# A decoder layer: the third part of the attention weights kept in memory, and the first batch's weight work moved to other engines

## The chip, the cores and the metric

The kernel runs on one core of a Trainium2 chip. The metric is device time in microseconds (us), as a median of three runs. A profile comes from one further execution and has its own time. The engines are named as in the profile: PE is TensorE, which multiplies matrices (PEld its weight loads, which overlap with it); DVE is VectorE; ACT is ScalarE; POOL is GpSimd; SP is SyncE, which here only issues transfers (DMAs). DMAs are carried by 16 DMA engines, whichever engine issued them: SP's are in queue q1 of the profile, ACT's in q10, POOL's in q0. When a line says L209, it is line 209 of the kernel before.

## The reference

The layer is computed for 4 batches of 512 rows with 512 columns, in float32. Cut to what matters:

```python
x = x + attention(layernorm(x))          # 16 heads of 128; Wq, Wk, Wv: [512, 2048], Wo: [2048, 512]
x = x + gamma * cross(layernorm(x), ctx) # 8 heads of 64 with softmax over 512 columns, no weights
x = x + ffn(layernorm(x))                # hidden size 1365; w1, w3, w2 made ternary with a mean-|w| scale
```

Inside the attention each head's score matrix is 128 x 128 (the sequence is contracted away), softmax runs over its last axis, and `att @ v` is turned back and multiplied with `Wo`. The change concerns the attention's weights alone.

## The kernel before

**Attention, by batch and by head group.** Batches run one after the other. Within a batch there are four head groups j, of four heads each. A group does four products in this order: `pu` (the rows of x against Wo), `py` (the Gram matrix G of x against Wk), `pm` (Wv against the result u of `pu`) and the scores `sc` (Wq against the result y of `py`). Softmax (`e`), its transpose (`pe`, evicted as `eT`) and the output product `po` of group j run inside group j+1: `pe` in the middle of `py`, `po` after it (`midway` and `output` in the loop at L637).

**The first batch is different from the others.** Batch 0 multiplies plain float32 weights (`products_f32`, L275). `first_weights` (L197) loads them in four chunks of 128 rows, as 512-byte pieces for q, k and v and as 2 KB rows for o. From each chunk of q, k and v it subtracts the last row of the weight matrix, which it has loaded as a broadcast tile `last`; this is a POOL operation, L209. The last row of the last chunk is then overwritten with the bias by a 2 KB load, L212, which waits for L209.

`keep_weights` (L216) cuts each chunk t of k, v and o into a high part h = t x constant (ACT, L223) and a low part l = t - S x h (DVE, L225) and stores both: h from ACT's queue (L224), l from POOL's queue (L226). A chunk of q is stored as it is, from ACT's queue (L219). That makes 24 + 4 stores of 256 KB a head group.

Batches 1 to 3 use the parts in three faster products (`products`, L242): h with h, l with l, and a difference part d with d. `weights` (L228) loads h and l on SP's queue and remakes d = l - h on POOL (L236). Products of h and l come first and that of d after them, for two row blocks at a time.

**Buffers.** Chunks and parts share a ring of 18 tiles of 256 KB (`a_w`, L134), so a load waits until the tile that lies 18 back is no longer used. In the first batch the parts h and l lie in a pool of six buffers each (`first`, L622). Its memory is given to the cross attention's input pool afterwards: the first loads of that pool (`keys`, L528) wait for all of the first pool's stores, and the loads of batch 1's x follow them on SP's queue.

**Evictions.** `evict` (L310) copies a PSUM bank to SBUF, in turn on ACT (L313) and DVE (L315). It is used by the products of batch 0 and by the Gram matrix of every batch.

**Order of the work.** The framework lays out each engine's instructions when the kernel is built, and an engine runs its own list strictly in order: an instruction that waits holds up everything behind it on that engine, transfers in its queue too. In the built list ACT has the copies of G and u behind the h of the next group's o chunk, which waits for that chunk's load. Within the attention of batches 1 to 3, steps of the preceding batch's cross attention and of the ternary quantization (`abs_w`, `tern_w`) are put in between by ticks; the first loads of the quantization are listed within batch 0. The FFN comes last and is not touched.

Of the kernel before, what the change touches and what calls it, by code (L numbers as in the profile page):

```python
# [10 lines left out]
F32 = mybir.dt.float32  # L11

F32R = mybir.dt.float32r
BF16 = mybir.dt.bfloat16
AF = mybir.ActivationFunctionType
ALU = mybir.AluOpType
AX = mybir.AxisListType

P = 128
B, T, D = 4, 512, 512  # L20
NC = T // P
KC = D // P
DH = 128
NG, HG = 4, 4
GW = HG * DH
# [7 lines left out]
S = 4096.0  # L33
H_OF = 1.0 - 0.5**13
# [3 lines left out]
def decoder_layer_kernel(  # L38
# [16 lines left out]
    nc = tc.nc  # L55
# [74 lines left out]
    def apool(name, bufs):  # L130
        return apools.enter_context(tc.tile_pool(name=name, bufs=bufs))
# [4 lines left out]
    yp, stp, tp = apool("a_y", 5), apool("a_stage", 2), apool("a_t", 3)  # L136
# [3 lines left out]
    kept_q = [dram.tile([D, GW], F32, name=f"kept_q_{j}") for j in range(HG)]  # L140
    kept = {
        (n, j, part): dram.tile([D, GW], F32, name=f"kept_{n}{part}_{j}")
        for n in "kvo"
        for j in range(HG)
        for part in "hl"
    }

    class Side:
# [29 lines left out]
    def load(dst, src):  # L178
        nc.sync.dma_start(dst, src)
        return dst  # L180

    def wtile(name, dt=F32R):
        return wp.tile([P, GW], dt, tag="w", name=name)

    w_of = {"q": wq, "k": wk, "v": wv}

    def heads(t):
        return t.rearrange("p (g c) -> p g c", g=NG)

    def of_heads(w, j):  # L190

        return w[:, :, ts(j, DH)].rearrange("g p c -> p g c")

    def by_group(rows, g):
        return rows.rearrange("(p g) d -> g p d", g=NG)[g]

    def first_weights(n, j, first):  # L197

        if n != "o":
            last = first.tile([P, GW], F32, tag="last", bufs=2, name=f"{n}_last_{j}")  # L200
            load(heads(last), of_heads(w_of[n][:, D - 1 : D, :], j).to_broadcast([P, NG, DH]))
        chunks = []
        for k in range(KC):
            t = wtile(f"{n}_raw_{j}_{k}", F32)
            if n == "o":
                load(t, by_group(wo[j * T : (j + 1) * T, :], k))
            else:
                load(heads(t), of_heads(w_of[n][:, ts(k, P), :], j))
                nc.gpsimd.tensor_tensor(t, t, last, ALU.subtract)  # L209
                if k == KC - 1:  # L210
                    bias = bqkv[:, ts(KINDS.index(n), GW)].rearrange("(o g) c -> g o c", o=1)
                    load(heads(t[P - 1 : P, :]), of_heads(bias, j))  # L212
            chunks.append(t)
        return chunks

    def keep_weights(n, j, chunks, first):  # L216
        for k, t in enumerate(chunks):
            if n == "q":
                nc.scalar.dma_start(kept_q[j][ts(k, P), :], t)  # L219
                continue  # L220
            h = first.tile([P, GW], F32R, tag="h", name=f"{n}_h_{j}_{k}")
            l = first.tile([P, GW], F32R, tag="l", name=f"{n}_l_{j}_{k}")
            nc.scalar.mul(h, t, H_OF / S)  # L223
            nc.scalar.dma_start(kept[n, j, "h"][ts(k, P), :], h.bitcast(F32))  # L224
            nc.vector.scalar_tensor_tensor(l, h.bitcast(F32), -S, t, ALU.mult, ALU.add)  # L225
            nc.gpsimd.dma_start(kept[n, j, "l"][ts(k, P), :], l.bitcast(F32))  # L226

    def weights(n, b, j):  # L228
        if n == "q":
            return [load(wtile(f"q_{b}_{j}_{k}", F32), kept_q[j][ts(k, P), :]) for k in range(KC)]  # L230
        tris = []
        for k in range(KC):
            tri = Tri(*(wtile(f"{n}{p}_{b}_{j}_{k}") for p in "hld"))
            load(tri.h.bitcast(F32), kept[n, j, "h"][ts(k, P), :])
            load(tri.l.bitcast(F32), kept[n, j, "l"][ts(k, P), :])
            nc.gpsimd.tensor_tensor(  # L236
                tri.d, tri.l.bitcast(F32), tri.h.bitcast(F32), ALU.subtract
            )
            tris.append(tri)
        return tris  # L240

# [33 lines left out]
    def products_f32(name, lhs, rhs, done, midway=None):  # L275

        for i in range(4):
            if i == 2 and midway:
                midway()
            p = bank(f"{name}_{i}")  # L280
            for k in range(4):
                nc.tensor.matmul(  # L282
                    p, lhsT=lhs(k)[:, ts(i, P)], rhs=rhs(k), start=(k == 0), stop=(k == 3)
                )
            done(i, p)
# [19 lines left out]
            tris.append(tri)  # L305
        return xs, tris

    turn = [0]

    def evict(dst, src):  # L310
        turn[0] += 1
        if turn[0] % 2:
            nc.scalar.copy(dst, src)  # L313
        else:
            nc.vector.tensor_copy(dst, src)  # L315

    def gram_upper(b, xs):
        if b == 0:
# [17 lines left out]
    def gram_rest(b, G):  # L336

        for rows in ((1, 2), (3,)):
            pt = bank(f"gt_{b}_{rows[0]}")
            n = 0  # L340
            for j in rows:
                for i in range(j):
                    nc.tensor.transpose(pt[:, ts(n + i, P)], G[i][:, ts(j, P)], ident)
                evict(G[j][:, : j * P], pt[:, n * P : (n + j) * P])
                n += j
        tris = []
        for m in range(KC if b > 0 else 0):
            tri = Tri(*(g3p.tile([P, D], F32R, name=f"g{p}_{m}") for p in "hld"))
            tri_of(tri, G[m])
            tris.append(tri)  # L350
        return tris
# [71 lines left out]
    def turned(b, j, e):  # L423
        eT = ep.tile([P, NG, DH], F32, tag="eT", bufs=2, name=f"eT_{b}_{j}")
        transpose_blocks(eT, e, f"pe_{b}_{j}", True)
        return eT

    def output(b, j, eT, ms, accs):
        for g in range(NG):
            po = bank(f"po_{b}_{j}_{g}")  # L430
            nc.tensor.matmul(po, lhsT=eT[:, g, :], rhs=ms[g], start=True, stop=True)  # L431
            if b == 0:
                nc.vector.tensor_tensor(accs[g], po, accs[g], ALU.add)
            else:
                nc.vector.scalar_tensor_tensor(accs[g], po, S * S, accs[g], ALU.mult, ALU.add)
            if j == HG - 1:
                (nc.gpsimd if b == B - 1 else nc.sync).dma_start(by_group(x_a[b], g), accs[g])
# [184 lines left out]
    first = first_pools.enter_context(tc.tile_pool(name="first", bufs=6, side="right"))  # L622
    cpools = ctx.enter_context(ExitStack())

    def accumulators(b):
        accs = []
        for g in range(NG):
            acc = accp.tile([P, D], F32, tag="acc", name=f"acc_{b}_{g}")
            load(acc, by_group(x[b], g))
            nc.gpsimd.tensor_tensor(acc, acc, bo_bc, ALU.add)  # L630
            accs.append(acc)
        return accs
# [4 lines left out]
    for j in range(HG):  # L637
        us, ys, ms = {}, {}, {}

        def to(tiles, pool, tag, name):  # L640
            def done(i, p):
                tiles[i] = pool.tile([P, 512], F32, tag=tag, name=f"{name}_{i}")
                evict(tiles[i], p)

            return done

        def midway():
            if waiting:
                waiting[2] = turned(*waiting[:3])

        w = first_weights("o", j, first)
        products_f32(
            f"pu_0_{j}", lambda c: xs[c], lambda c: w[c], to(us, u3p, "u3", f"u_0_{j}")
        )
        if j == 0:
            gram_rest(0, G)
        keep_weights("o", j, w, first)
        w = first_weights("k", j, first)
        products_f32(
            f"py_0_{j}", lambda e: G[e], lambda e: w[e], to(ys, yp, "y", f"y_0_{j}"), midway  # L660
        )
        keep_weights("k", j, w, first)
        if waiting:
            output(*waiting)
        w = first_weights("v", j, first)
        products_f32(f"pm_0_{j}", lambda k: w[k], lambda k: us[k], to(ms, mp, "m", f"m_0_{j}"))
        keep_weights("v", j, w, first)
        w = first_weights("q", j, first)
        e = scores(0, j, w, ys)
        keep_weights("q", j, w, first)  # L670
        if j == 0:
            load(bo_bc, bo.to_broadcast([P, D]))
            load(gam, gamma.to_broadcast([P, 1]))
            accs = accumulators(0)
        if j == HG - 1:
            xs, x3 = normed(1, False)
        waiting = [0, j, e, ms, accs]
# [8 lines left out]
    for b in range(1, B):  # L686
# [10 lines left out]
        for j in range(HG):  # L697
# [3 lines left out]
            ys = keys_of(b, j, g3, weights("k", b, j), tick)  # L701
# [62 lines left out]
    for i in range(NHC):  # L764
        r = min(P, HID - i * P)
# [3 lines left out]
    for b in range(B):  # L769
# [3 lines left out]
        for i in range(NHC):  # L773
# [4 lines left out]
            r = min(P, HID - i * P)  # L778
# [25 lines left out]
        for c in range(NC):  # L804
# [3 lines left out]
            for i in range(NHC):  # L808
                r = min(P, HID - i * P)
# [59 lines left out]
```

## Time and profile before

| | us |
|---|---|
| median of 3 runs (lowest to highest) | 1261.23 (1254.18 to 1262.58) |
| the profiled execution: its time / its span | 1263.35 / 1261.6 |
| batch 0 of the attention, to the end of its last `po` | 0 to 253 |
| batches 1 to 3 with cross attention and quantization | 253 to 950 |
| FFN | 950 to 1262 |

| stretch | PE busy | DVE | ACT | POOL | granted PE clock | DMA share | GB/s |
|---|---|---|---|---|---|---|---|
| 0 to 64 us | 37.4 | 31.4 | 15.7 | 33.6 | 0.81 | 0.96 | 324 |
| 64 to 119 us | 52.4 | 20.3 | 14.3 | 21.9 | 1.00 | 0.79 | 257 |
| 119 to 253 us | 133.0 | 57.3 | 32.2 | 47.5 | 0.99 | 0.60 | 197 |
| 253 to 950 us | 674.1 | 502.2 | 259.6 | 204.2 | 0.99 | 0.60 | 196 |
| 950 to 1262 us | 305.3 | 151.5 | 132.7 | 24.5 | 1.00 | 0.16 | 53 |

Busy times are in us. "DMA share" is the mean over the 16 DMA engines: one engine busy alone gives 1/16. A DMA shows in the profile as packets, one for each contiguous piece, with small ones for its end markers; packets are counted by size. "Busy" for PE says that a matmul was in the pipe, not that PE was at its peak. Lines of waits read: who waited <- for whom: us in total, times, the longest.

### The profile page before, as it was taken

To read this page: it belongs to the slowest core of one execution; us is meant where nothing else is said; L and a number is where in the kernel's file an instruction comes from. 1 tells how busy PE (TensorE), PEld (TensorE's weight loads), DVE (VectorE), ACT (ScalarE), POOL (GpSimd) and SP (SyncE) were. 2 spreads that over 40 slices of the span, in tenths; PEclk is the share of its full clock that TensorE was granted. 3 is DMA by queue.
4 is the path that set the end of the run, shared out by engine and by line. 5 is a ranking of instruction groups with operands and counts; after the bars stand their busy time and mean duration, and the time that the engine had idled before them with its cause. 6 is when DMAs were issued, how large, how long until landed. Compare 5 with 4: busy or idle time off the path is not lost.

```text
span 1261.6 us, 15663 instructions
## 1 busy us (share of the span) xinstructions
PE 1202.1 (95%) x5182; PEld 812.9 (64%) x5182; DVE 762.6 (60%) x1411; ACT 454.5 (36%) x948; POOL 331.6 (26%) x306
## 2 busy tenths in 40 slices
PE   7499999999999999999999999999999999999998
PEld 3153544577675666777675677776766666678786
DVE  6334336387786864975969475686856845635232
ACT  3113222134332432352334334332534836724020
POOL 5535343143321322432222243222302000000000
PEclk9699999999999999999999999999999999999999
DMA  9978675284476654743775374557765120020101
GB/s 311 334 243 292 234 242 198 81 269 150 147 230 214 196 167 147 255 151 131 230 244 178 128 243 150 168 199 241 238 212 188 42 75 26 9 92 17 53 15 51
DMA packets 137401, 214.19 MB, mean 170 GB/s; under 512 B 13156, under 2 KB 56212, under 8 KB 137320
## 3 DMA queue, kind: packets, MB, share of 16 engines
q1 hardware_dynamic: 122664, 178.58, 44.2%
q0 software_dynamic: 5440, 17.83, 3.9%
q10 hardware_dynamic: 9216, 16.78, 3.5%
q8 instruction: 41, 0.67, 0.2%
q14 instruction: 40, 0.33, 0.1%
HBM read 162.81 MB, written 50.33 MB: 169 GB/s over the span
## 4 chain that ended last, share of the span: by engine, by line
PE 79%; DMA 10%; DVE 6%; issue 2%; ACT 1%; POOL 1%; SPq 1%; ACTq 0%; DVEq 0%; POOLq 0%
PE h L784 13%; PE y L811 6%; PE xo L586 5%; PE xs L542 5%; PE sc L394 4%; PE xp L106 4%; PE py L282 4%; PE pm L282 3%; PE po L431 3%; PE pu L282 2%; PE pg L326 2%; DMA o_raw<-in_wo_dram 1%; DMA v_raw<-in_wv_dram 1%; PE pm_2h L249 1%; DMA kl<-kept_kl 1%
## 5 line engine op out<-in xcount | busy, mean ns | idle before, releaser
L784 PE MATMUL h<-fxh,t 128*128 128x512 f32 (+1 forms) x352 | 140.4, 401 | 0.8 <-ACT fxh L116 0.8
L784 PE MATMUL h<-fxl,t 128*128 128x512 f32 (+1 forms) x352 | 138.3, 395 | 0.0
L554 ACT ACTIVATE p<-xs,xnmax 128x512 f32<-128x512 f32 x128 | 87.0, 687 | 88.5 <-DVE xnmax L549 43.6
L236 POOL TENSOR_TENSOR od<-ol,oh 128x512 fp32r<-128x512 f32 x48 | 62.9, 1310 | 203.7 <-DMA ol<-kept_ol 56.1
L548 DVE TENSOR_REDUCE xnmax<-xs 128x1 f32<-128x512 f32 x128 | 83.9, 682 | 29.9 <-PE xs L542 29.7
L236 POOL TENSOR_TENSOR vd<-vl,vh 128x512 fp32r<-128x512 f32 x48 | 67.5, 1412 | 114.5 <-DMA vl<-kept_vl 66.2
L236 POOL TENSOR_TENSOR kd<-kl,kh 128x512 fp32r<-128x512 f32 x48 | 63.9, 1332 | 121.3 <-DMA kl<-kept_kl 67.3
L784 PEld LDWEIGHTS h<-fxh,t 128*128 128x128 f32 (+1 forms) x352 | 65.1, 185 | 20.0 <-issue 1.5
L542 PE MATMUL xs<-keys,qs 64*128 64x512 f32 x256 | 75.9, 641 | 0.8 <-DVE u L270 0.8
L784 PEld LDWEIGHTS h<-fxl,t 128*128 128x128 f32 (+1 forms) x352 | 65.0, 185 | 15.7
L106 PE MATMUL xp<-ident,p 128*128 128x128 f32 x512 | 66.9, 275 | 4.2 <-DVE u L270 4.2
L566 DVE TENSOR_SCALAR p<-p,xrden 128x512 f32<-128x512 f32 x128 | 68.3, 575 | 3.0
L106 PEld LDWEIGHTS xp<-ident,p 128*128 128x128 f32 x512 | 59.1, 141 | 16.5 <-DVE u L270 4.7
L811 PE MATMUL y<-t,gh 128*128 128x512 f32 (+1 forms) x176 | 69.5, 395 | 0.0
L811 PE MATMUL y<-t,gl 128*128 128x512 f32 (+1 forms) x176 | 68.8, 391 | 0.0
L118 POOL CAST gh<-gf 128x512 fp32r<-128x512 f32 (+1 forms) x24 | 14.8, 616 | 197.1 <-DVE gf L795 174.1
L431 PE MATMUL po<-m,eT 128*128 128x512 f32 x128 | 60.3, 614 | 6.3 <-ACT eT L109 5.7
L586 PE MATMUL xo<-pt,vals 128*64 128x512 f32 x256 | 63.7, 599 | 2.5 <-ACT pt L109 2.4
L282 PE MATMUL py<-k_raw,G 128*128 128x512 f32 x128 | 60.4, 626 | 4.3 <-issue 4.3
L109 ACT COPY pt<-xp 128x512 f32<-128x512 f32 x96 | 53.4, 593 | 27.1 <-PE xp L106 27.1
L795 DVE SCALAR_TENSOR_TENSOR gf<-h,scales_w,sl 128x512 f32<-128x512 f32 (+1 forms) x44 | 32.9, 747 | 47.2 <-PE h L784 39.3
L282 PE MATMUL pu<-o_raw,xn 128*128 128x512 f32 x128 | 55.6, 592 | 0.0
(215 smaller groups left out, 2559.2 us busy)
## 6 DMA issues: line engine op xcount, KB each, us to landing
oh<-kept_oh SPq DMA_DIRECT2D x48, 256.0 KB
ol<-kept_ol SPq DMA_DIRECT2D x48, 256.0 KB
kh<-kept_kh SPq DMA_DIRECT2D x48, 256.0 KB
kl<-kept_kl SPq DMA_DIRECT2D x48, 256.0 KB
vh<-kept_vh SPq DMA_DIRECT2D x48, 256.0 KB
vl<-kept_vl SPq DMA_DIRECT2D x48, 256.0 KB
q<-kept_q SPq DMA_DIRECT2D x48, 256.0 KB
t_w<-tern_w SPq DMA_DIRECT2D x24, 227.5 KB
```

The costliest lines, as they stand in the source:

```text
L106: nc.tensor.transpose(pt[:, ts(k, P)], src[:, ts(k, P)], ident)
L109: nc.scalar.copy(dst, pv)
L236: nc.gpsimd.tensor_tensor(tri.d, tri.l.bitcast(F32), tri.h.bitcast(F32), ALU.subtract)
L282: nc.tensor.matmul(p, lhsT=lhs(k)[:, ts(i, P)], rhs=rhs(k), start=(k == 0), stop=(k == 3))
L431: nc.tensor.matmul(po, lhsT=eT[:, g, :], rhs=ms[g], start=True, stop=True)
L542: nc.tensor.matmul(sc, lhsT=qs[rows, ts(m, P)], rhs=keys[rows, :], start=True, stop=True)
L548: nc.vector.reduce_max(nmax[:, j : j + 1], scs[j], axis=AX.X)
L554: nc.scalar.activation(p, scs[j], AF.Exp, bias=nmax[:, j : j + 1], scale=xscale, accum_out=den[:, j : j + 1],)
L566: nc.vector.tensor_scalar(ps[j], ps[j], rden[:, j : j + 1], None, ALU.mult)
L586: nc.tensor.matmul(po[rows, :], lhsT=vals[:, l, rows], rhs=pt[j][:, l, :], start=(l == 0), stop=(l == NC - 1),)
L784: nc.tensor.matmul(ph[:r, :], lhsT=t[:, k, i * P : i * P + r], rhs=fxT[j][:, k, :], start=(k == 0 and j == 0), stop=(k == KC - 1 and j == 1),)
L811: nc.tensor.matmul(py, lhsT=g[i][j][:r, ts(c, P)], rhs=t2[:r, i, :], start=(i == 0 and j == 0), stop=(i == NHC - 1 and j == 1),)
```

## The change

Four things are done at once.

- `keep_weights` also makes d = l - h and stores it, and `weights` loads d as it loads h and l. POOL no longer remakes it.
- In batch 0, the subtraction of the last row, h, l and d are all DVE operations. The h and l operations of `keep_weights` are followed by stores that all go out from POOL's queue, q's too.
- `evict` always uses ACT.
- In head group 1 two one-column DVE copies take both buffers of the quantization's staging pool, after y is there. Its loads (`abs_w`) wait for them.

One thing more follows from the order of the bias: the last chunk of q, k and v is loaded as 127 rows and one row, and the subtraction runs on 127 rows. The bias load no longer waits for a subtraction.

In the built lists, a head group of batch 0 now has 40 stores on POOL's queue (12 h, 12 l, 12 d, 4 q) and none on ACT's; a head group of batches 1 to 3 has 40 loads on SP's queue, where it had 28, each d behind its h and l.

```diff
@@ -142,7 +142,7 @@
         (n, j, part): dram.tile([D, GW], F32, name=f"kept_{n}{part}_{j}")
         for n in "kvo"
         for j in range(HG)
-        for part in "hl"
+        for part in "hld"
     }
 
     class Side:
@@ -205,25 +205,33 @@
             if n == "o":
                 load(t, by_group(wo[j * T : (j + 1) * T, :], k))
             else:
-                load(heads(t), of_heads(w_of[n][:, ts(k, P), :], j))
-                nc.gpsimd.tensor_tensor(t, t, last, ALU.subtract)
-                if k == KC - 1:
+                r = P if k < KC - 1 else P - 1
+                load(heads(t[:r, :]), of_heads(w_of[n][:, k * P : k * P + r, :], j))
+                if r < P:
                     bias = bqkv[:, ts(KINDS.index(n), GW)].rearrange("(o g) c -> g o c", o=1)
-                    load(heads(t[P - 1 : P, :]), of_heads(bias, j))
+                    load(heads(t[r:, :]), of_heads(bias, j))
+                nc.vector.tensor_tensor(t[:r, :], t[:r, :], last[:r, :], ALU.subtract)
             chunks.append(t)
         return chunks
 
     def keep_weights(n, j, chunks, first):
+        def keep(name, part):
+            nc.gpsimd.dma_start(name[ts(k, P), :], part)
+
         for k, t in enumerate(chunks):
             if n == "q":
-                nc.scalar.dma_start(kept_q[j][ts(k, P), :], t)
+                keep(kept_q[j], t)
                 continue
-            h = first.tile([P, GW], F32R, tag="h", name=f"{n}_h_{j}_{k}")
-            l = first.tile([P, GW], F32R, tag="l", name=f"{n}_l_{j}_{k}")
-            nc.scalar.mul(h, t, H_OF / S)
-            nc.scalar.dma_start(kept[n, j, "h"][ts(k, P), :], h.bitcast(F32))
-            nc.vector.scalar_tensor_tensor(l, h.bitcast(F32), -S, t, ALU.mult, ALU.add)
-            nc.gpsimd.dma_start(kept[n, j, "l"][ts(k, P), :], l.bitcast(F32))
+            h, l, d = (
+                first.tile([P, GW], F32R, tag=p, name=f"{n}_{p}_{j}_{k}").bitcast(F32)
+                for p in "hld"
+            )
+            nc.vector.tensor_scalar(h.bitcast(F32R), t, H_OF / S, None, ALU.mult)
+            keep(kept[n, j, "h"], h)
+            nc.vector.scalar_tensor_tensor(l.bitcast(F32R), h, -S, t, ALU.mult, ALU.add)
+            keep(kept[n, j, "l"], l)
+            nc.vector.tensor_tensor(d.bitcast(F32R), l, h, ALU.subtract)
+            keep(kept[n, j, "d"], d)
 
     def weights(n, b, j):
         if n == "q":
@@ -231,11 +239,8 @@
         tris = []
         for k in range(KC):
             tri = Tri(*(wtile(f"{n}{p}_{b}_{j}_{k}") for p in "hld"))
-            load(tri.h.bitcast(F32), kept[n, j, "h"][ts(k, P), :])
-            load(tri.l.bitcast(F32), kept[n, j, "l"][ts(k, P), :])
-            nc.gpsimd.tensor_tensor(
-                tri.d, tri.l.bitcast(F32), tri.h.bitcast(F32), ALU.subtract
-            )
+            for p in "hld":
+                load(getattr(tri, p).bitcast(F32), kept[n, j, p][ts(k, P), :])
             tris.append(tri)
         return tris
 
@@ -305,14 +310,8 @@
             tris.append(tri)
         return xs, tris
 
-    turn = [0]
-
     def evict(dst, src):
-        turn[0] += 1
-        if turn[0] % 2:
-            nc.scalar.copy(dst, src)
-        else:
-            nc.vector.tensor_copy(dst, src)
+        nc.scalar.copy(dst, src)
 
     def gram_upper(b, xs):
         if b == 0:
@@ -672,6 +671,11 @@
             load(bo_bc, bo.to_broadcast([P, D]))
             load(gam, gamma.to_broadcast([P, 1]))
             accs = accumulators(0)
+        if j == 1:
+
+            for i in range(2):
+                held = stp.tile([P, 512], F32, tag="stage", name=f"held_{i}")
+                nc.vector.tensor_copy(held[:, 0:1], ys[i][:, 0:1])
         if j == HG - 1:
             xs, x3 = normed(1, False)
         waiting = [0, j, e, ms, accs]
```

## The prediction

> **What bounds the kernel now.** First the page: span, slices and DMA packets.
>
> ```profile
> span 1261.6 us, 15663 instructions
> ...
> PE   7499999999999999999999999999999999999998
> ...
> PEclk9699999999999999999999999999999999999999
> DMA  9978675284476654743775374557765120020101
> ...
> DMA packets 137401, 214.19 MB, mean 170 GB/s; under 512 B 13156, under 2 KB 56212, under 8 KB 137320
> ```
>
> PE is busy in nearly every slice; only the first two are thin, and there the DMA engines are full. So what can be won lies in batch 0. The waits of 0 to 64 us say what PE lacks there:
>
> ```profile
> ACT o_h L223 <- DMA o_raw<-in_wo_dram: 18.1, 4, 11.3
> ...
> PE gt L343 <- ACT G L313: 13.9, 1, 13.9
> ```
>
> ACT stands before the h of the next group's o chunk until that chunk lands, and the copies of G stand behind it; PE waits 13.9 us, and 4.3 more for the next copy. The stretches by engine confirm it (us, then busy us of PE, PEld, DVE, ACT, POOL, then clock, DMA share, GB/s):
>
> ```profile
> 35.00:49.00 14.00, 0.18 (x1) 0.00 (x0) 2.05 (x4) 1.95 (x4) 8.54 (x8) 0.61 0.97 343
> ...
> 140.00:190.00 50.00, 50.00 (x155) 25.08 (x154) 19.97 (x30) 13.37 (x28) 23.92 (x26) 1.00 0.78 255
> ```
>
> From 119 us on PE has no gap. A head group then takes 48.6 us (the chain has `pu` at 142.05 and again at 190.69). In batches 1 to 3 PE idles 23 of 697 us, shared among many small waits:
>
> ```profile
> PE pm_2h L249 <- DVE acc L435: 4.4, 3, 2.9
> ...
> PE py_0h L249 <- DMA kh<-kept_kh: 4.1, 3, 1.8
> ```
>
> **The change part by part.** The working is against the profiled execution: 1263.35 us, 1.75 over its span and 2.1 over the median.
>
> *ACT is freed.* The h operations (48 x 0.63 = 30 us) and 64 DMA issues leave ACT; the copies of G then follow PE directly. The 13.9 and 4.3 us go: -18 at most.
>
> *POOL and DVE.* POOL loses 48 subtractions (64.1 us, L209) and 144 remakes (194.3 us, L236). It gains 48 stores, and 64 come from ACT: 40 a head group at 0.56 us (L226) = 22 us. DVE gets, by head group, 12 x (0.69 for l by L225 + 0.54 for h by L100 + 2 x 0.69 for subtraction and d by L172) = 31 us, and keeps some 7 for `po` and softmax, against PE's 48.6. This is hidden under PE as long as its inputs arrive. DVE executes in order: an h that waits for a store of six chunks ago holds up the next chunk's subtraction, and then PE.
>
> *Batches 1 to 3.* 144 more loads of 256 KB on SP, 37.7 MB in 697 us: 196 GB/s becomes 250, below the 324 to 343 seen. Each d load waits in SP's queue until PE leaves the old d tile, and the next chunk's h and l are behind it. In group 1 of batch 1 the load of the fourth kh would issue near 309, not at 305.68, and is needed at 314.4; `kl` took 3.7 to 4.2 us to land where PE waited for it, so a margin of 1 to 2 us is left. If that cover fails, 36 products lose up to 0.5 us each: +18. Against it, DVE is rid of POOL's operations beside it (L172 takes 0.78 us here, 0.68 where POOL is quiet). PE's waits for DVE are some 15 us in all; I take back a third. The gram's evictions, now all on ACT, follow PE at 0.6 us. Sum -3, between -15 and +18.
>
> *The 127-row loads.* The largest term, and the diff's smallest line. How many DMA engines carry a load? Two rows of the list of DMAs are of odd shape:
>
> ```profile
> abs_w<-in_w2t_dram SPq DMA_DIRECT2D x1, 170.0 KB
> ...
> k_raw<-in_bqkv_dram SPq DMA_DIRECT2D x4, 2.0 KB
> ```
>
> The first is one of four 85-row DMAs, the second the bias: one row, four pieces. If each engine that took part leaves one small packet at the end, the 809 other 128-row DMAs on the three queues leave 16 x 809 = 12944, and `gam` 128 four-byte pieces and 16. Of the page's 13156 under 512 B, 68 remain for 12 bias loads and four of 85 rows. From 200.7 to 201.4 us one bias load is alone in q1:
>
> ```profile
> DMA packets 34, 0.06 MB, mean 82 GB/s; under 512 B 15, under 2 KB 19, under 8 KB 34
> ...
> q1 hardware_dynamic: 8, 0.00, 1.3%
> ```
>
> Eight packets: its 19 - 15 = 4 pieces and 4 markers. So 12 x 4 = 48, and 20 remain: 5 for each 85-row DMA. The number of engines is then 16 for 128 rows, 4 for 4, 5 for 85, each time the largest divisor up to 16. 127 is prime: one engine. The trace has no such load, so the ends are sixteen engines (0.8 us) and one.
>
> [...]
>
> What one engine moves in such pieces shows from 171.6 to 173.2 us, where only 512-byte pieces are moving:
>
> ```profile
> DMA packets 1060, 0.53 MB, mean 330 GB/s; under 512 B 29, under 2 KB 1060, under 8 KB 1060
> ```
>
> 330 / 16 = 20.6 GB/s an engine; 127 x 2 KB = 260 KB take 12.6 us. The other end is the mean of 0 to 250 us:
>
> ```profile
> q1 hardware_dynamic: 40336, 30.69, 41.6%
> q10 hardware_dynamic: 9216, 16.78, 17.8%
> ```
>
> q10's 64 stores took 17.8% of 16 x 250 us, 11.1 engine-us each, 0.69 on each engine. q1's 1664 engine-us, less 44.5 loads at 11.1 and 14 quantization loads at 9.9, leave 1030 for 60 of these: 17.2 each, with contention. I take 12.6, the row of pure traffic.
>
> Bill of the loaded engine by head group: three 127-row loads 37.8; nine other chunks and three broadcasts, 12 x 0.8 = 9.6; four o loads and 40 stores, 44 x 0.69 = 30.4. Sum 77.8 us, against 40 if spread and PE's 48.6. Four groups 311; x, `acc`, `bo` and batch 1's x, 13 x 0.69 = 9; 14 quantization loads 9; start 3: 332. Less 10 for the last stores, behind which no product waits; with the first slices' share of 0.96 the last q chunk lands at 322 / 0.95 = 339. Then subtraction and `sc` (4 us), the wait of batch 1's x behind the stores with its normalization (7 more), gram, `pe` and `po` (13.5): the last `po` of batch 0 ends at 364, not 253. **+111**, from +94 (no slack) to +162 (17.2 a load). The 18 us from ACT are within: PE waits for loads anyhow. Its clock falls in gaps (0.61 above), but even at half clock a product of 13.7 us fits in the 26 us between two chunk sets.
>
> Sum: 1263.35 + 111 - 3 = 1371; I say 1370.
>
> **The rivals.**
>
> *The short load spreads out* (faster, the other side). For it: nothing here shows 127 rows. Against: 85 rows went to 5 engines; a split by remainder would use 16. Then a group moves 59 x 256 KB = 15.5 MB, 47 us at 330 GB/s, below PE's 48.6; the G stall goes (-18), stores that gate DVE return 3: 1263 - 15 - 3 = 1245. By the bill above, 40 + 37.8/k on k engines, it decides from k = 5 on.
>
> *The stores' queue is the limit.* POOL issues 40 stores in order, each waiting for parts from DVE. At 0.56 us they take 22 us a group; were each delayed by one DVE operation of 0.69, 50 us, just over PE's 48.6. That eats the gain: 1260, about as before. For it: all stores in one queue. Against: issues lasted 0.54 to 0.69 us while DVE was running.
>
> [...]
>
> *The one engine is slower still*: 17.2 us a load and every d load late: 1263 + 162 + 15 = 1440.
>
> **How the numbers follow.** One engine, in the bill's range: 0.88, of which 0.06 for the last rival. Spread out: 0.08. Store queue: 0.04. The time is the bill's, 1370. Low end: 1263 + 94 - 15 = 1342, less 32 because loads may overlap better with stores than one bill allows; high end 1440. 1310 to 1440 leaves out both small rivals and some tail. Faster by over 1% (what a measurement of this kernel can just tell): 0.08; within 1%: 0.04; slower: 0.88.
>
> **What the profile after would show.** Under 512 B: 13156 + 16 x 192 new DMAs - 12 x 15 = 16048 if 127 rows take one engine, 16228 if sixteen. Batch 0 with a DMA share well below 0.96 while PE idles, its gaps ended by the fourth chunk of k, v and q, three times a group; `po` of the groups 75 to 90 us apart. No wait for G behind o_h. No L236; loads of d beside h and l, and PE's waits for them under 10 us. I am wrong if the gaps end with DVE behind stores, or if batch 0 ends before 253.

## The result, and the profile after

The changed kernel takes 1380.51 us (median of 4 runs, 1379.01 to 1384.17); the kernel before took 1261.90 beside it (1254.18 to 1263.97). The ratio is 1.0949, with a 95% interval of 1.0901 to 1.0997: it is **slower by 9.5%**, 119 us. The forecast was 1370, from 1310 to 1440.

The page of the changed kernel, with the rows that answer to those shown of before: span, then the 40 slices of TensorE, of its granted clock and of the DMA engines, then the packets.

```profile
span 1380.1 us, 15677 instructions
...
PE   7862185383999999999999999999999999999998
...
PEclk9986597697899999999999999999999999999999
DMA  6674455664477677769667776957796412002101
...
DMA packets 157652, 264.50 MB, mean 192 GB/s; under 512 B 16048, under 2 KB 59056, under 8 KB 157572
```

Three things are to be seen. The gaps of TensorE lie in the first ten slices (34.5 us each), all within batch 0; behind them the row is nines. In these same slices the DMA engines are only four to seven tenths busy, where they were seven to nine tenths busy in the first four before: TensorE lacks data while the DMA engines, taken together, have time. And the packets under 512 bytes are exactly the 16048 that the prediction had worked out for a 127-row load on one engine (sixteen engines would have left 16228).

Stretches by engine tell it in time (from:to, us, then busy us of PE, PEld, DVE, ACT, POOL, then clock, DMA share, GB/s). Two lie in batch 0, the third covers batches 1 to 3:

```profile
0.00:64.00 64.00, 48.68 (x120) 23.07 (x121) 29.81 (x71) 10.95 (x22) 19.69 (x39) 0.95 0.63 211
...
119.00:200.00 81.00, 35.52 (x95) 16.94 (x94) 30.83 (x61) 9.80 (x22) 22.11 (x40) 0.71 0.56 194
...
395.00:1071.00 676.00, 667.90 (x3154) 472.84 (x3153) 451.07 (x932) 261.98 (x618) 18.46 (x16) 1.00 0.75 255
```

Of the 81 us from 119 to 200, which TensorE filled before (80.65), it now works 35.5, at a clock of 0.71. The DMA share there is 0.56.

Where batch 0 ends can be read from the last addition of a head group's output (`acc<-po`). It starts at 252.8 us before and at 393.8 after: +141. From there to the last such addition of batch 3 it is 699.7 us before (to 952.5) and 677.2 after (to 1071.0): -22.5. The rest, 309 us, is the same. So the change costs 141 us in batch 0 and brings back 22.5 in the other batches, 118.5 together by the two profiled executions.

What TensorE waits for in batch 0 (us in all, times, longest):

```profile
PE pe L106 <- DVE e L417: 99.7, 3, 43.8
PE py L287 <- DVE k_raw L213: 13.0, 1, 13.0
PE sc L393 <- DVE q_raw L213: 11.1, 1, 11.1
...
PE pm L287 <- DVE v_raw L213: 6.8, 1, 6.8
```

No wait for G is left. Three of these four name a subtraction on a chunk, and the first names the softmax rows `e`, which stand behind the q subtractions on VectorE; what VectorE itself waits for in this time is the landing of q_raw (64.6 us), k_raw (60.5) and v_raw (59.1).

### The profile page after: what moved, and what is told of

Same layout as the page of the kernel before. It is cut to its first block, busy times and chain, and to the rows that moved or that the text cites. A ratio compares the mean times of both kernels' runs of the same rounds, so it can differ in the third digit from the quotient of the medians.

```text
span 1380.1 us, 15677 instructions
## 1 busy us (share of the span) xinstructions
PE 1210.4 (88%) x5182; PEld 817.4 (59%) x5182; DVE 748.6 (54%) x1519; ACT 443.8 (32%) x938; POOL 139.1 (10%) x226
## 2 busy tenths in 40 slices
DMA packets 157652, 264.50 MB, mean 192 GB/s; under 512 B 16048, under 2 KB 59056, under 8 KB 157572
## 4 chain that ended last, share of the span: by engine, by line
PE 72%; DMA 19%; SPq 4%; DVE 3%; issue 1%; ACT 1%; DVEq 0%
PE h L788 12%; DMA q_raw<-in_wq_dram 7%; PE y L815 6%; PE xs L541 5%; SPq L179 4%; PE xo L585 4%; PE po L430 4%; PE xp L106 4%; PE sc L393 4%; DMA k_raw<-in_wk_dram 3%; DMA v_raw<-in_wv_dram 3%; PE pg L325 2%; DMA k_raw<-in_bqkv_dram 2%; PE pm L287 2%; PE py L287 2%; DMA kl<-kept_kl 1%
## 5 line engine op out<-in xcount | busy, mean ns | idle before, releaser
L106 PE MATMUL pe<-ident,e 128*128 128x128 f32 x64 | 11.5, 305 | 100.7 <-DVE e L417 100.7
L287 PE MATMUL py<-k_raw,G 128*128 128x512 f32 x128 | 64.4, 661 | 13.0 <-DVE k_raw L213 13.0
L629 POOL TENSOR_TENSOR acc<-acc,bo_bc 128x512 f32<-128x512 f32 x16 | 21.4, 1358 | 502.6 <-DMA acc<-in_x_dram 492.8
L106 PEld LDWEIGHTS pe<-ident,e 128*128 128x128 f32 x64 | 8.1, 149 | 107.5 <-issue 104.8
L287 PE MATMUL pu<-o_raw,xn 128*128 128x512 f32 x128 | 61.7, 641 | 11.4 <-DVE acc L432 10.6
L406 ACT ACTIVATE e<-sc,nmax 128x128 f32<-128x128 f32 x64 | 22.7, 369 | 137.0 <-DVE nmax L402 137.0
L287 PE MATMUL pm<-u,v_raw 128*128 128x512 f32 x128 | 57.6, 608 | 6.8 <-DVE v_raw L213 6.8
```

Source lines behind the costliest of these rows:

```text
L106: nc.tensor.transpose(pt[:, ts(k, P)], src[:, ts(k, P)], ident)
L287: nc.tensor.matmul(p, lhsT=lhs(k)[:, ts(i, P)], rhs=rhs(k), start=(k == 0), stop=(k == 3))
```

## The experiments

The theory is the prediction's: a load of 127 rows runs on one DMA engine, and this engine's bill sets batch 0. Its rivals are that VectorE's new work or GpSimd's store queue costs the time, and, from the trace after, that SyncE's queue does. In that trace SyncE's issues look like this (start, us):

```profile
32.59 20.11 SPq L179 DMA_DIRECT2D v_raw<-in_bqkv_dram  x1
52.74 0.44 SPq L179 DMA_DIRECT2D q_raw<-in_wq_dram  x1
53.31 0.42 SPq L179 DMA_DIRECT2D q_last<-in_wq_dram  x1
53.78 2.29 SPq L179 DMA_DIRECT2D q_raw<-in_wq_dram  x3
56.11 21.59 SPq L179 DMA_DIRECT2D q_raw<-in_bqkv_dram  x1
```

Most issues take 0.4 to 0.8 us, but the one that follows a 127-row load (the bias row's) takes 20 here (11.7 to 24.1 in all twelve cases), and no other load is issued meanwhile.

This table is the overview. Ratios are against runs of the kernel before that were taken beside each, whose medians were 1259.8 to 1262.0. The ends and lengths are those of one profiled execution, read as above; where runs spread, it can lie some us from the median.

| kernel | median us | ratio, 95% | batch 0 ends | batches 1 to 3 |
|---|---|---|---|---|
| before | 1261.9 | 1 | 252.8 | 699.7 |
| changed | 1380.5 | 1.095 (1.090 to 1.100) | 393.8 | 677.2 |
| changed, 112 + 15 rows | 1238.8 | 0.982 (0.978 to 0.985) | 251.1 | 676.0 |
| changed, 128 rows, bias over them | 1233.2 | 0.978 (0.975 to 0.982) | 250.2 | 675.1 |
| changed, 122 + 5 rows | 1298.5 | 1.029 (1.025 to 1.034) | 314.1 | 677.8 |
| changed, 124 + 3 rows | 1261.0 | 0.999 (0.997 to 1.002) | 273.3 | 674.0 |
| before, with 127-row loads alone | 1380.8 | 1.095 (1.091 to 1.099) | 373.1 | 700.2 |
| changed, 127-row loads from ScalarE's queue | 1370.0 | 1.087 (1.083 to 1.091) | 384.5 | 675.0 |
| changed, two orders mended | 1370.6 | 1.088 (1.084 to 1.091) | 382.3 | 675.6 |
| 128 rows, d not kept | 1241.0 | 0.984 (0.979 to 0.990) | 226.5 | 693.1 |
| 128 rows, d stored in batch 1 | 1234.5 | 0.980 (0.976 to 0.984) | 231.9 | 692.8 |
| 128 rows, no held copies | 1230.5 | 0.974 (0.970 to 0.978) | 244.6 | 676.2 |
| 128 rows, held copies in group 3 | 1223.1 | 0.968 (0.965 to 0.971) | 234.2 | 675.1 |
| the same, square root later | 1220.8 | 0.966 (0.963 to 0.969) | 235.7 | 675.2 |

### Only the row count of the load

First the load is cut in two, 112 and 15 rows:

```diff
-                load(heads(t[:r, :]), of_heads(w_of[n][:, k * P : k * P + r, :], j))
+                cuts = (0, P) if r == P else (0, 112, r)
+                for a, z in zip(cuts, cuts[1:]):
+                    load(heads(t[a:z, :]), of_heads(w_of[n][:, k * P + a : k * P + z, :], j))
```

> The changed kernel, with only the 127 rows of the last chunk loaded as 112 and 15 rows, so that 16 and 15 DMA engines may carry them; all else of the change is kept. Theory (the loads on one engine are the whole loss): batch 0 shrinks from 394 us to 240 to 255, batches 1 to 3 keep the 22 us that they gained, and the time is 1220 to 1250; packets under 512 B rise from 16048 to about 16048 + 12 x (16 + 15 - 1) = 16408. Rival (the subtraction and h on VectorE, or all stores from GpSimd's queue, cost the time): 1300 or more, with VectorE or the stores ending the gaps of batch 0.

Second, all 128 rows are loaded and the bias row is put over the last one, as before:

```diff
-                load(heads(t[:r, :]), of_heads(w_of[n][:, k * P : k * P + r, :], j))
+                load(heads(t), of_heads(w_of[n][:, ts(k, P), :], j))
```

> The changed kernel, with the last chunk loaded as 128 rows and the bias row put over its last row by a second DMA, as in the kernel before; subtraction still on 127 rows on VectorE. Theory (one engine): 1220 to 1255, like the split into 112 and 15 rows, or a few us more because the bias load now waits for the 128-row load to land; packets under 512 B about 16228. Rival (VectorE or GpSimd's queue): 1300 or more.

Measured: 1238.81 and 1233.23 us, both as the theory had it; the first leaves 16408 packets under 512 B, the number expected for 16 and 15 engines. Everything else of the change is in both, so VectorE's work and the stores from GpSimd's queue cost nothing like 140 us. Both rivals fall. The second kernel's packets, from its page, and its stretches:

```profile
DMA packets 157880, 264.53 MB, mean 214 GB/s; under 512 B 16228, under 2 KB 59284, under 8 KB 157800
```

```profile
0.00:64.00 64.00, 54.84 (x158) 27.59 (x159) 42.32 (x93) 12.11 (x24) 35.11 (x61) 1.00 1.01 347
...
119.00:200.00 81.00, 77.36 (x225) 39.70 (x223) 55.42 (x107) 14.40 (x36) 34.14 (x61) 0.96 0.94 326
```

The packets are the sixteen-engine count. TensorE works 77 of the 81 us, and the DMA engines are full: 1.01 and 0.94. The two kernels differ by 5.6 us; what makes the cut a little dearer no run shows.

The other way round, the kernel before gets the 127-row load and nothing else of the change:

```diff
-                load(heads(t), of_heads(w_of[n][:, ts(k, P), :], j))
-                nc.gpsimd.tensor_tensor(t, t, last, ALU.subtract)
-                if k == KC - 1:
+                r = P if k < KC - 1 else P - 1
+                load(heads(t[:r, :]), of_heads(w_of[n][:, k * P : k * P + r, :], j))
+                if r < P:
...
-                    load(heads(t[P - 1 : P, :]), of_heads(bias, j))
+                    load(heads(t[r:, :]), of_heads(bias, j))
+                nc.gpsimd.tensor_tensor(t[:r, :], t[:r, :], last[:r, :], ALU.subtract)
```

> The kernel before, with only the load of the last chunk changed: 127 rows and the bias row beside them instead of 128 rows and the bias row over the last one; GpSimd still subtracts (127 rows), ScalarE still makes h and stores from its queue, d is remade. Theory (one engine): batch 0 grows by 95 to 145 us, the time is 1355 to 1410. Rival (the loss is in VectorE or GpSimd's queue): within 10 us of the kernel before, 1250 to 1272.

Measured: 1380.84 us. The twelve loads alone make the whole loss; batch 0 ends at 373.1 instead of 252.8. Its packets under 512 B fall to 13156 - 12 x 15 = 12976, as the count says:

```profile
DMA packets 137173, 214.17 MB, mean 155 GB/s; under 512 B 12976, under 2 KB 55984, under 8 KB 137092
```

That this is the time of the changed kernel is chance: that one has 20.7 us more in batch 0, where its one engine carries its part of 48 d stores as well (0.69 us each by the prediction's bill), and 23.0 less behind it.

### How many engines

The same cut, at 122 and at 124 rows instead of 112:

> The changed kernel, with the 127 rows loaded as 122 and 5 rows: if the largest divisor up to 16 sets the number, 2 and 5 engines. By the bill of the prediction a head group then takes 40 + 37.8 / 2 = 59 us of the most loaded engine against 48.6 of TensorE: 10 us too long in four groups, so 40 to 60 us above the split into 112 and 15 rows: 1265 to 1300. If any two parts are as good as each other (what counts is only that no part is a prime number of rows): the time of the split into 112 and 15 rows, within 10 us. If the engine count is not the cause: 1380.

> The changed kernel with the 127 rows loaded as 124 and 3 rows: 4 and 3 engines if the largest divisor up to 16 sets the number. The prediction's bill gives 40 + 37.8 / 4 = 49.4 us a head group for the most loaded engine, 0.8 over the 48.6 of TensorE: 1240 to 1260, against 1239 for 112 and 15 rows (16 and 15 engines) and 1298 for 122 and 5 rows (2 and 5). If the engine count were not what sets the loss, and the row count of the larger part were: as 122 and 5 rows, 1290 to 1305. Packets under 512 B: 16048 + 12 x (4 + 3 - 1) = 16120.

Measured: 1298.48 and 1260.96 us, the second just over the upper end of what was expected. Both kernels leave the same number of small packets (by the largest divisor up to 16, 2 + 5 and 4 + 3 engines, both 7), so the packets agree with the prediction's count but can't tell the two apart:

```profile
DMA packets 157724, 264.50 MB, mean 211 GB/s; under 512 B 16120, under 2 KB 59128, under 8 KB 157644
```

The time does. 122 and 124 rows are 37 us apart, which no cost by size or number of DMAs would give; what differs, by that divisor, is how many engines carry the large part, 2 or 4. The prediction's bill for the most loaded engine was 40 + 37.8/k us a head group. Four groups, divided by the share of 0.95 that the prediction used, give 80 us from k = 1 to 2 and 40 us from k = 2 to 4; batch 0 ended at 393.8, 314.1 and 273.3, which is 79.7 and 40.8 less. From there to 112 rows it is 22.2 us more, where the bill against TensorE's own 48.6 us a group left 3: with the two limits nearly equal, this kernel took more than the larger of them; why was not tried. The bill let the loaded engine outlast TensorE up to k = 4. That k = 4 takes just the time of the kernel before (0.9994) does not follow from it: there, what the rest of the change gains and what the load still costs cancel.

All runs here agree with the count that the prediction worked out from the trace before, the largest divisor of the rows up to 16: 127 rows on 1, 122 on 2, 124 on 4, 112 and 128 on 16. For 127 (16048), 112 (16408) and 128 rows (16228) the packets under 512 B show it, for the other two the packets (16120 in both) and the ends of batch 0 (314.1 and 273.3 us) together.

### The engine or the queue

The twelve loads are issued from ScalarE's queue, so that SyncE's is free for all others:

```diff
-                load(heads(t[:r, :]), of_heads(w_of[n][:, k * P : k * P + r, :], j))
+                queue = nc.sync if r == P else nc.scalar
+                queue.dma_start(heads(t[:r, :]), of_heads(w_of[n][:, k * P : k * P + r, :], j))
```

> The changed kernel with its 127-row loads, but these 12 loads issued from ScalarE's queue; everything else stays in SyncE's. It asks whether the loss comes from the one engine that carries the load or from SyncE's queue, which issued nothing for some 20 us after each such load. Theory (the engine's own 77.8 us a head group): within 20 us of 1380. Rival (the held queue): the other loads now run ahead, and the time falls below 1320.

Measured: 1370.0 us, 10.5 less than the changed kernel: with SyncE's queue free of these loads, less than a tenth of the loss goes. But the long issue went along with the load. ScalarE's timeline, loads and copies:

```profile
12.67 20.36 ACTq L210 DMA_DIRECT2D v_raw<-in_wv_dram  x1
33.07 0.58 ACT L315 COPY G<-pg 128x512 f32<-128x512 f32 x1 [23.20 <-PE pu L288]
33.13 23.31 ACTq L210 DMA_DIRECT2D q_raw<-in_wq_dram  x1
...
56.48 0.54 ACT L315 COPY G<-pg 128x256 f32<-128x256 f32 x2 [22.44 <-issue]
```

Now ScalarE stands 20 and 23 us at an issue behind an earlier 127-row load, and the copies of G wait behind it; TensorE waits 22.4 us for G in this kernel. So the time of this run does not show what the held queue would cost on an engine with nothing else to do.

Its third head group shows the other side, one-engine loads without the hold. There the three issues, and the first of the next group, last 0.21 us:

```profile
175.19 0.21 ACTq L210 DMA_DIRECT2D k_raw<-in_wk_dram  x1
...
202.49 0.21 ACTq L210 DMA_DIRECT2D v_raw<-in_wv_dram  x1
...
225.60 0.21 ACTq L210 DMA_DIRECT2D q_raw<-in_wq_dram  x1
...
262.10 0.21 ACTq L210 DMA_DIRECT2D k_raw<-in_wk_dram  x1
```

In SyncE's queue the longest single issue of this stretch takes 0.61 us. Still 86.9 us pass from one k load to the next, and the k and q loads take 27.4 and 26.1 us to land; in the changed kernel, where the three issues after the loads of this group are held 12 to 17 us, the group takes 81.9 (from one k bias issue to the next). So the held queue is not needed for the loss, and as its whole cause the rival falls.

What the DMA engines did can be counted from the traces' packets. From 10 to 344 us of the changed kernel, just one packet is under way in 31% of the time and none in 2%. With ScalarE's queue (10 to 334 us) it is 31% and 2% as well; with 128-row loads (10 to 200 us) one packet alone is 0.4% and none does not occur. So for 31% of batch 0's loading time one engine at most is at work and fifteen have no packet, whichever queue issued the load.

### Why the end of batch 0 is so late

The last q chunk landed at 344.1 us, and 49.7 us passed before the last addition of batch 0. The prediction had 25. The chain that ended last, from that chunk on:

```profile
322.11 22.01 DMA q_raw<-in_wq_dram
...
344.84 0.21 DVE e L417
...
346.79 5.08 DMA xn<-in_x_dram
...
354.44 0.31 ACT std_a L92
...
357.11 0.60 ACT eT L109
...
357.76 5.26 PE po L430 x8
363.01 13.73 PE pm L287 x32
376.75 3.57 PE sc L393 x32
380.32 8.63 PE pg L325 x32
...
390.06 3.70 PE po L430 x8
```

`po` of group 2 and `pm` of group 3, 19 us of products, come only now, although the v chunks had landed. On VectorE the softmax rows of group 2 stand behind the q subtraction. On ScalarE the square root of batch 1's statistics, for which x has to be loaded, stands ahead of `eT`, the turned rows that `po` reads. The experiment mends both orders, each with a copy of one column that makes the later one depend on the other:

```diff
+            if behind is not None and k == 0:
+                nc.vector.tensor_copy(t[:, 0:1], behind[:, GW - 1 : GW])
...
-        w = first_weights("q", j, first)
+        w = first_weights("q", j, first, e)
...
+        if behind is not None:
+            nc.vector.tensor_copy(mv[:, 0, 0:1], behind)
...
-            xs, x3 = normed(1, False)
+            xs, x3 = normed(1, False, ys[3][:, 0:1])
```

> The changed kernel with its 127-row loads, and two instructions' order changed: in every group the softmax rows of the group before come ahead of the subtractions of the q chunks on VectorE, and the square root of batch 1's statistics comes behind the y copies of group 3 on ScalarE. It asks why 49.6 us and not 25 passed from the landing of the last q chunk to the end of batch 0. Theory (po of group 2 and pm of group 3 were held up by these two orders, although their data were there): 20 to 27 us less, 1353 to 1362. Rival (the DMAs behind the q chunk, batch 1's x and the stores, set the tail): within 8 us of 1380.

Measured: 1370.61 us, 10 less, between the two expectations. The chain of this kernel:

```profile
332.33 18.39 DMA q_raw<-in_wq_dram
...
353.93 6.62 DMA xn<-in_x_dram
...
362.53 0.59 DVE acc L436
...
363.16 5.63 PE sc L397 x32
368.79 8.63 PE pg L329 x32
377.42 0.45 PE pe L106 x4
...
378.53 3.70 PE po L434 x8
```

`po` and `pm` are gone from the chain, and from the landing of the q chunk (350.7) to the last addition (382.3) it is 31.6 us instead of 49.7. So the mechanism is shown, with 18 us of the tail. But the copy that holds the q load back also made its landing 6.6 us later, and `sc` now waits for an `acc` addition that stands behind the statistics of x on VectorE: a third order of the same kind. The gain that is left is 11.5 us in batch 0.

### What the rest of the change is worth

On the kernel with 128-row loads, d is neither made nor stored in batch 0, and GpSimd remakes it in batches 1 to 3 as before:

```diff
-            nc.vector.tensor_tensor(d.bitcast(F32R), l, h, ALU.subtract)
-            keep(kept[n, j, "d"], d)
...
-            for p in "hld":
+            for p in "hl":
                 load(getattr(tri, p).bitcast(F32), kept[n, j, p][ts(k, P), :])
+            nc.gpsimd.tensor_tensor(tri.d, tri.l.bitcast(F32), tri.h.bitcast(F32), ALU.subtract)
```

> The changed kernel with the 128-row loads (the second experiment), and without the third part in memory: d is neither made nor stored in batch 0, and GpSimd remakes it in batches 1 to 3 as in the kernel before. It asks which part of the change gave batches 1 to 3 their 23 us. Theory (GpSimd's 144 remakes, which ran beside VectorE's operations, were the price there): batches 1 to 3 go from 675 back to 690 to 700 us, while batch 0, which the DMA engines fill to 0.98, loses 48 stores of 0.69 us an engine and shrinks from 250 to 232 to 245: together 1229 to 1252. Rival (the evictions on ScalarE gave it): batches 1 to 3 stay at 675 and the time is 1215 to 1228.

Measured: 1241.0 us (1231.0 to 1246.2, a wider spread than the others; the profiled execution was the shortest). In the profiled execution both halves went the way that the theory had them. Batches 1 to 3 take 693.1 us, 18.0 more than with d in memory; batch 0 ends at 226.5, 23.7 earlier and below the 232 to 245 expected. These two would make the kernel 6 us faster than the one with d, but by the medians it is 8 us slower (1241.0 against 1233.2): the profiled execution lies 10 us under its median, so each of the two sizes is uncertain by some 10 us. By these traces, of the 24.6 us that batches 1 to 3 gain with 128-row loads, 18.0 come from d, and 6.6 from the rest; what in the rest was not tried (the evictions of the gram, now all on ScalarE, are what else changed there).

The groups of VectorE in batches 1 to 3 show how GpSimd's remakes cost time (busy us, mean ns). First the changed kernel, without them:

```profile
L565 DVE TENSOR_SCALAR p<-p,xrden 128x512 f32<-128x512 f32 x96 | 42.3, 484 | 2.6
...
L172 DVE TENSOR_TENSOR ul<-u,uh 128x512 fp32r<-128x512 f32 x48 | 32.8, 684 | 0.3 <-ACT uh L171 0.3
```

And this experiment, with them:

```profile
L566 DVE TENSOR_SCALAR p<-p,xrden 128x512 f32<-128x512 f32 x96 | 56.0, 624 | 2.1
L173 DVE SCALAR_TENSOR_TENSOR ud<-uh,ul 128x512 fp32r<-128x512 f32 x48 | 40.5, 844 | 0.2
L172 DVE TENSOR_TENSOR ul<-u,uh 128x512 fp32r<-128x512 f32 x48 | 35.7, 743 | 0.5 <-ACT uh L171 0.4
```

The same operations take 484 ns without GpSimd's work and 624 with it, 684 and 743. In the kernel before they took 605 and 809. VectorE as a whole is busy 451 us in the changed kernel's batches 1 to 3 and 504 in the kernel before. It is single operations that grow: of the 96 in the first row the shortest, median and longest take 470, 482 and 1535 ns with the remakes, and 469, 481 and 492 in the kernel with 128-row loads and d in memory. What holds them up no row of a trace names.

Next, d is stored later: batch 1 remakes it on GpSimd and stores it, batches 2 and 3 load it.

```diff
-            nc.vector.tensor_tensor(d.bitcast(F32R), l, h, ALU.subtract)
-            keep(kept[n, j, "d"], d)
...
-            for p in "hld":
+            for p in "hld" if b > 1 else "hl":
                 load(getattr(tri, p).bitcast(F32), kept[n, j, p][ts(k, P), :])
+            if b == 1:
+                nc.gpsimd.tensor_tensor(tri.d, tri.l.bitcast(F32), tri.h.bitcast(F32), ALU.subtract)
+                nc.gpsimd.dma_start(kept[n, j, "d"][ts(k, P), :], tri.d.bitcast(F32))
```

> The changed kernel with the 128-row loads, and d stored in another batch: batch 0 keeps h and l alone, batch 1 remakes d on GpSimd and stores it, batches 2 and 3 load it. Theory (batch 0 is bound by the DMA engines, and d costs it 12.6 MB; later there is room): batch 0 shrinks from 250 to 232 to 245 us, batch 1 pays 5 to 8 us for its remakes, 1222 to 1236 against 1233. Rival (batch 0 is bound by the products and waits that the DMAs don't set): batch 0 stays at 250, and the time is 1236 to 1245.

Measured: 1234.5 us, no gain. Batch 0 shrinks as expected, by 18.3 us, but batches 1 to 3 grow by 17.7. Nearly all of it is in batch 1: by the first store of a batch's result it takes 246.0 us, against 228.5 with d loaded and 235.0 with d remade and not stored. Why the store costs 11 us more there wasn't settled; TensorE's waits in it are small and spread out (3.5 us the longest).

Last, the loads that batch 0 need not have. The changed kernel holds back twelve loads of the feed-forward weights until group 1 by two copies. Without the copies:

```diff
-        if j == 1:
-
-            for i in range(2):
-                held = stp.tile([P, 512], F32, tag="stage", name=f"held_{i}")
-                nc.vector.tensor_copy(held[:, 0:1], ys[i][:, 0:1])
```

> The changed kernel with the 128-row loads, without the two copies that hold back the quantization loads: 12 loads of 228 KB and their VectorE sums then come in group 1 and earlier. It asks whether these copies, the part of the change that no step of the prediction priced, are worth anything. Theory (the engines are full in batch 0 wherever the loads stand): within 4 us of 1233. Rival (they keep the first groups' weight loads in time): 1238 to 1245.

Measured: 1230.53 us, against 1233.23 with them; the intervals overlap, and the copies in group 1 are worth nothing that shows. In group 3 they are:

```diff
-        if j == 1:
+        if j == HG - 1:
```

> The changed kernel with the 128-row loads, and the two copies that hold back the loads of the feed-forward weights for their quantization made in group 3 instead of group 1, so that these 12 loads of 228 KB leave batch 0. Theory (batch 0 is bound by its DMA engines, 0.94 to 1.01 busy up to 200 us): 12 x 0.65 = 8 us less in batch 0, and batches 1 to 3, where the engines are 0.77 busy, pay at most 3: 1224 to 1231 against 1233. Rival (batch 0 is bound by waits and orders that these loads don't set, as storing d later gave nothing in the sum): 1231 to 1240.

Measured: 1223.12 us, 10 less. Batch 0 ends 16.0 us earlier, and batches 1 to 3 stay at 675.1; the two profiled executions lie 16.1 apart and the medians 10.1, where the loads' own time would give 8. With the square root's order mended as well (the second half of the order experiment):

> The kernel of the experiment before this one, and besides the square root of batch 1's statistics put behind the y copies of group 3 on ScalarE. Theory (eT of group 2 and po behind it waited 6.9 us for the square root there): 3 to 7 us below the experiment before, 1218 to 1228. Rival (the next order, the last statistics on VectorE, takes the place of that wait): the same time as the experiment before.

Measured: 1220.76 us. The wait for `eT` that this was to take away, 7.6 us in all at 128 rows, is 0.7, but it was only 1.5 in the experiment before already. The 2.4 us between the medians lie within the spread of runs, and by the traces batch 0 is no shorter, so the rival stands. What TensorE waits for in its batch 0 is little:

```profile
PE pg L327 <- DVE xn L308: 8.9, 1, 8.9
PE pe L106 <- DVE e L419: 8.0, 1, 8.0
PE po L432 <- ACT eT L109: 0.7, 1, 0.7
```

This kernel has the lowest median of the study, with no clear distance to the one before it: 0.966 of the kernel before (0.963 to 0.969), 160 us below the changed one.

## Why the prediction was right, and where it was off

**One engine for 127 rows** was the step that carried the forecast, and it holds: by the count of small packets (16048, and 12976 in the kernel before with these loads alone), by that kernel's time (1380.8 us), and by the ends of batch 0 for 1, 2 and 4 engines (393.8, 314.1 and 273.3). Nothing in the trace before showed such a load; the prediction worked the count out from two DMAs of odd shape and the packets of the page.

**The bill of the loaded engine** said that the last q chunk lands at 339 us. It landed at 344.1. Where it took the pure 12.6 us a load, single loads take 16 to 28 us in the chain; the likely reason, not tried alone, is that the same engine carried stores and other chunks meanwhile. Even so, the sum over all of an engine's work came within 5 us of the landing. Two slips stand in its working: it names a share of 0.96 and divides by 0.95, worth 4 us, and by the same division 17.2 us a load gives +169, not the +162 of the upper bound. The output products of groups 0 and 3 start at 178.3 and 390.1 in the chain, 70.6 us a group on the mean, below the predicted 75 to 90; up to `po` of group 2, at 357.8, it is 90 us a group, and the last one follows 32 us later because group 2's was late.

**The end of batch 0** was mis-sized. The prediction let it come at 364, 25 us behind the q chunk: subtraction and `sc`, the wait for x, gram, `pe` and `po`. It took 49.7, to 393.8. The step took for granted that `po` of group 2 and `pm` of group 3 would be done while TensorE waited for the chunk. Both stood behind it by the order of two other engines. The order experiment took 18 of these 25 us away.

**Batches 1 to 3** were mis-sized the other way: -3 forecast (from -15 to +18), -22.5 measured. The cover that the prediction doubted held: TensorE's waits for `kh` and `kl` are 1.0 us there, so the 144 more loads cost no wait to speak of. What was too small is the term for VectorE without GpSimd beside it. I had taken back a third of TensorE's named waits for VectorE, 5 us. The experiment without d in memory puts d at 18 by its trace, with the uncertainty said there. TensorE's idle time there, 23 us before, is 8 after, and the prediction's list of named waits held only part of it.

The two errors, +29.8 at the end of batch 0 and -19.5 behind it, stand against each other, so that the forecast of 1370 is nearer to 1380.5 than its terms are (111 forecast and 141 measured for batch 0). That closeness is luck.

**ACT freed**, forecast at -18 within the bill: the wait for G is gone. What that alone is worth no run shows. With 128 rows and no d, batch 0 ends 26.3 us earlier than before, by all of the change in batch 0 together (ScalarE, VectorE's subtraction, the stores' queue, the held loads). With the d stores, 2.6 us of this are left, as the DMA engines are then full (1.01 and 0.94 of 0 to 64 and 119 to 200 us with 128 rows).

**The rivals.** The spread load was forecast at 1245 and took 1238.8 and 1233.2; its condition is false for 127 rows. The store queue as the limit is refuted: the stores' issues take 0.54 to 0.68 us in the changed kernel, by the mean of each group, and all of them are in the kernels at 0.98. That each store is delayed by one VectorE operation of 0.69 us, as the rival supposed, no run shows. Single issues do last longer beside a `TENSOR_SCALAR` of VectorE, as the making of h now is:

```profile
121.90 1.10 POOL L219 DMA_DIRECT2D kept_kd<-k_d  x1 [0.21 <-issue]
122.12 0.76 DVE L229 TENSOR_SCALAR v_h<-v_raw 128x512 fp32r<-128x512 f32 x2
```

Of the 160 store issues of batch 0, 18 last longer than 0.56 us, up to 1.10. In every one of the 18 VectorE runs a `TENSOR_SCALAR`, and the 124 issues without one beside them take 0.55 at most; what holds the 18 up no row tells. In all they add 5.6 us to GpSimd's queue, far too little to be the limit here. The third rival, d loads late, did not come.

## What to carry to other kernels

Read a load's row count before its size. One row fewer turned sixteen engines into one here and cost 119 us; 122 rows cost 37, 124 nothing, and loading all 128 rows and writing the last one again gained 28. When an engine's total work sets the end, sum all that it carries, and then read what stands behind the last arrival on every engine's queue, since that tail was as wrong in this prediction as the sum was right. Work given to an idle engine can still be dear: beside GpSimd's remakes VectorE's operations took up to 29% longer on the mean (624 ns against 484).

## What the runs showed that was not expected

The issue of the DMA that follows a one-engine load in the same queue takes 11.7 to 24.1 us on SyncE in the changed kernel, instead of mostly 0.4 to 0.8. On ScalarE six of the twelve issues took 10.6 to 23.6 us, and its copies waited that long. No step of the prediction had it. Moving the loads to the other queue changed the time by only 10.5 us, and a group without held issues was no shorter; what the hold costs by itself stays open.

Keeping d in memory is worth less than it looks from either side: by the traces the loads save 18 us in batches 1 to 3, and the stores cost 24 in batch 0, where the DMA engines are full (1.01 and 0.94 with 128 rows). By the medians, keeping d is still a gain of 8 us (1233.2 against 1241.0).
